# Taking 16 transposes a pair out of a four-layer graph network, and ordering its work anew with the port of GpSimd and VectorE in the plan

## The chip, the cores and the metric

One core of a Trainium2 chip. The metric is device microseconds (us) of one execution; medians of several executions are given. An execution can fall into a slower state with a lower clock. The granted TensorE clock is a share of full speed, so 1 is full. In the profile PE is TensorE's matmuls, PEld its weight loads, DVE VectorE, ACT ScalarE, POOL GpSimd, SP the engine that issues the loads. `L761` is line 761 of the kernel's file; the new kernel is longer, so its lines have other numbers.

## The reference, cut to what matters

Four residual layers on 64 graphs of 256 nodes and 256 features, fp32. The kernel works on pairs of graphs, 32 of them.

```python
h = relu(layernorm(x)); x = x + attention8(h, adj)      # layer 0: 8 heads, softmax over neighbours
h = relu(layernorm(x)); x = x + elu(gat(h, adj))        # layer 1
h = relu(layernorm(x)); x = x + gated_graph(h, adj)     # layer 2: 3 steps of a GRU cell
h = relu(layernorm(x)); x = x + gat4(h, adj)            # layer 3: 4 heads, softmax
# layer 2, one step:
m = h @ weight[i]; aggr = A.T @ m
r = sigmoid(i_r + h_r); z = sigmoid(i_z + h_z)
n = tanh(i_n + r * h_n);  h = (1 - z) * n + z * h
```

## The kernel before

The kernel lists its work as tasks (engine, expected us, what to do) and a small planner in the kernel's own file orders all tasks of all 32 pairs at build time, so that softmax and layernorm of one pair run beside the matmuls of others. After that the order on each engine is fixed.

```python
# Plan.order, at each step: the task that can begin first (cut)
for engine, us, do in t.forms:
    begin = max(start, free.get(engine, 0.0))
    for x in t.before:      # HOP, SAME: delay of a hand-over to another or to the same engine
        begin = max(begin, x.end + (self.HOP if x.engine != engine else self.SAME)[x.engine])
    key = (round(begin, 3), (t.layer == 2) == (engine == "PE"), t.pair, t.order)
...
"w4": (20, [P, T * D], FP, 6),      # 20 buffers; a pair that isn't the oldest must leave 6 of them free
```

Layer 0 leaves the softmax rows undivided and divides the context product. For that the reciprocals of the row sums are widened, transposed on TensorE (8 transposes a pair), copied out and multiplied in:

```python
rzw() <- rz() widened to 128 x 256                             # VectorE
nc.tensor.transpose(psz()[...], rzws[ti]()[:, cc] ..., ident)  # 4 a graph
nc.scalar.copy(rzT(), psz())
nc.vector.tensor_tensor(cT ..., psc, rzT, ALU.mult)
```

Each step of layer 2 has features on the partitions. The state after it is transposed to tokens (8 transposes a pair and step), after the last step as well, only to be added to `x`.

## Time and profile before

| | before |
|---|---|
| median of the first 3 runs | 4326.13 us (4325.0 to 4328.71) |
| TensorE busy | 98% |
| VectorE, ScalarE, GpSimd busy | 68%, 53%, 14% |
| granted TensorE clock, mean | 0.996 |

Most lines are in the prediction below. The list of who waited for whom on TensorE, where the first columns are the waiting group and the releaser, and the numbers are us in total, times, and the longest:

```profile
PE ps L278 <- DMA wih_sb<-in_L_gnn_w_ih_dram: 16.0, 1, 16.0
...
PE ps L909 <- ACT w L494: 10.1, 4, 5.3
...
PE ps L457 <- issue: 7.2, 1, 7.2
```

The profile's "idle" counts a gap only where no record is under way, and records overlap; so I use a second measure. **Work** is count times usual start-to-start time, summed over TensorE's groups; **waits** are what is left between the first and the last matmul. In the prediction I put the work at 4157; I had taken the mean for the context product (L614), and 10 of its 64 blocks hold a wait of 1.15 us inside. With the undisturbed 1.864 us a block it is 4147 of work and 156 of waits, and that is used from here on. (Another reading of "usual" moves some 10 us between the two columns in every kernel alike; the differences between kernels are what counts.)

### The profile page before, as it was taken

The page shows a single profiled execution, that of the slowest core. Times are in us where ns is not written, and L with a number is a line of the kernel's source. Part 1 is how long each engine was busy: PE and PEld are TensorE (multiplying, and loading weights), DVE is VectorE, ACT ScalarE, POOL GpSimd, SP SyncE. Part 2 cuts the span into 40 slices and gives each one's busy share as a digit, 9 for nine tenths or more (in the row PEclk, how much of TensorE's full clock was granted, in tenths as well). Part 3 has the DMA queues.
Part 4 walks back from the last instruction along what each step waited for, and adds up shares of the span by engine and source line. Part 5 has one row for each costly group of instructions (what it writes and reads, how often), then busy time and mean ns, then how long its engine had stood idle before and what let it go on. Part 6 is the DMA issues. An engine that isn't in the chain of part 4 may idle for free.

```text
span 4324.5 us, 56216 instructions
## 1 busy us (share of the span) xinstructions
PE 4244.1 (98%) x20720; PEld 2631.3 (61%) x20720; DVE 2930.0 (68%) x5426; ACT 2301.1 (53%) x6105; POOL 590.3 (14%) x582
## 2 busy tenths in 40 slices
PE   7999999999999999999999999999999999999997
PEld 5665566656656665666566566656655665666564
DVE  6775577667657755876676577558765765776554
ACT  4664465545545644655455456446554554564444
POOL 1111111111111111111111111111111111111111
PEclk9999999999999999999999999999999999999999
DMA  2000011000000000010000000000100100000000
GB/s 83 21 18 22 20 36 34 20 16 24 30 25 25 13 28 25 30 35 20 11 30 30 25 25 13 27 25 26 40 11 17 32 30 25 25 13 28 15 15 15
DMA packets 109986, 108.47 MB, mean 25 GB/s; under 512 B 7312, under 2 KB 109712, under 8 KB 109712
## 3 DMA queue, kind: packets, MB, share of 16 engines
q1 hardware_dynamic: 109712, 104.89, 7.6%
q8 instruction: 163, 2.67, 0.3%
q14 instruction: 111, 0.91, 0.1%
HBM read 88.09 MB, written 16.78 MB: 24 GB/s over the span
## 4 chain that ended last, share of the span: by engine, by line
PE 77%; DVE 8%; issue 8%; ACT 5%; POOL 1%; SPq 0%; DMA 0%; POOLq 0%; ACTq 0%; DVEq 0%
PE ps L761 36%; PE ps L775 7%; PE ps L518 5%; PE ps L480 5%; PE ps L573 4%; PE ps L717 3%; PE ps L654 3%; PE ps L540 2%; PE ps L457 2%; PE ps L614 2%; PE ps L840 2%; PE ps L858 2%; ACT w L886 2%; ACT w L494 2%; DVE w L823 1%
## 5 line engine op out<-in xcount | busy, mean ns | idle before, releaser
L761 PE MATMUL ps<-w,whhT 128*128 128x512 f32 x2304 | 1080.3, 595 | 0.7 <-DVE w L402 0.4
L761 PE MATMUL ps<-w,giT 128*128 128x512 f32 x2304 | 1063.6, 593 | 0.0
L494 ACT ACTIVATE w<-w,mx 128x256 f32<-128x256 f32 x1664 | 825.7, 503 | 186.3 <-DVE mx L561 128.9
L401 ACT COPY w<-ps 128x512 f32<-128x512 f32 x983 | 553.0, 587 | 657.3 <-PE ps L775 290.8
L761 PEld LDWEIGHTS ps<-w,giT 128*128 128x128 f32 x2304 | 433.6, 190 | 523.9 <-issue 513.3
L761 PEld LDWEIGHTS ps<-w,whhT 128*128 128x128 f32 x2304 | 415.3, 190 | 406.6 <-issue 383.9
L811 POOL TENSOR_TENSOR w<-w,w 128x512 f32<-128x512 f32 x192 | 251.2, 1317 | 1689.6 <-ACT w L806 1331.8
L402 DVE COPY w<-ps 128x512 f32<-128x512 f32 x553 | 366.4, 684 | 153.7 <-PE ps L573 58.0
L786 ACT ACTIVATE w<-ps,brz 128x512 f32<-128x512 f32 x192 | 131.8, 687 | 463.2 <-PE ps L761 460.3
L791 DVE TENSOR_SCALAR w<-w 128x512 f32<-128x512 f32 x192 | 81.6, 425 | 407.8 <-ACT w L786 407.7
L554 DVE SCALAR_TENSOR_TENSOR w<-ps,mask 128x512 f32<-128x512 f32 x512 | 333.3, 680 | 33.9 <-PE ps L540 33.9
L775 PE MATMUL ps<-w,w 128*128 128x256 f32 x1536 | 355.7, 379 | 0.0
L775 PEld LDWEIGHTS ps<-w,w 128*128 128x128 f32 x1536 | 286.2, 190 | 60.7 <-issue 22.9
L494 ACT ACTIVATION_READ_ACCUMULATOR w<-w,mx 128x1 f32 x1664 | 322.9, 194 | 0.0
L823 DVE SCALAR_TENSOR_TENSOR w<-w,w 128x512 f32<-128x512 f32 x192 | 152.5, 794 | 246.3 <-ACT w L818 240.7
L561 DVE TENSOR_REDUCE mx<-w 128x4 f32<-128x1024 f32 x256 | 309.2, 1208 | 2.0
L573 PE MATMUL ps<-ident,w 128*128 128x128 f32 x2048 | 269.4, 273 | 0.6
L573 PEld LDWEIGHTS ps<-ident,w 128*128 128x128 f32 x2048 | 235.1, 140 | 57.1 <-issue 25.6
L818 ACT ACTIVATE w<-ps,brz 128x512 f32<-128x512 f32 x192 | 130.8, 681 | 235.0 <-PE ps L761 234.9
L424 POOL TENSOR_SCALAR rs<-mv 128x4 f32<-128x4 f32 x128 | 33.6, 262 | 1354.8 <-DVE mv L417 1293.5
L886 ACT ACTIVATE w<-w,f 128x256 f32<-128x256 f32 x512 | 217.1, 503 | 1.4
L445 DVE TENSOR_SCALAR w<-x,mv,rs 128x256 f32<-128x256 f32 x384 | 185.3, 541 | 16.5 <-POOL rs L425 15.8
(113 smaller groups left out, 5633.0 us busy)
## 6 DMA issues: line engine op xcount, KB each, us to landing
adj<-in_adj_dram SPq DMA_DIRECT2D x128, 512.0 KB, 4.1
x<-in_x_dram SPq DMA_DIRECT2D x64, 256.0 KB, 2.8
out_dram<-x SPq DMA_DIRECT2D x64, 256.0 KB, 2.2
gg_sb<-in_L_gnn_weight_dram SPq DMA_DIRECT2D x3, 256.0 KB, 3.7
wih_sb<-in_L_gnn_w_ih_dram SPq DMA_DIRECT2D x1, 768.0 KB, 6.9
whh_sb<-in_L_gnn_w_hh_dram SPq DMA_DIRECT2D x1, 768.0 KB, 8.6
wq_sb<-in_L_gnn_Wq_dram SPq DMA_DIRECT2D x1, 256.0 KB, 2.8
wk_sb<-in_L_gnn_Wk_dram SPq DMA_DIRECT2D x1, 256.0 KB, 3.0
```

Source lines behind the costliest of these rows:

```text
L401: (A, act(n), lambda: nc.scalar.copy(dst(), src())),
L402: (V, dve(n), lambda: nc.vector.tensor_copy(dst(), src())),
L480: mm(ps()[:, c * D : (c + 1) * D], chunk(src, k, 2 * g + c), rhs[:, k, :], start=k == 0, stop=k == 1)
L494: nc.scalar.activation(tok(e(), N)[:, i, :], tok(e(), N)[:, i, :], AF.Exp, bias=mx()[:, m : m + 1], accum_out=zs()[:, z : z + 1],)
L518: mm(ps(), w[:, k, o * P : (o + 1) * P], tok(hT(), N2)[:, k, :], start=k == 0, stop=k == 1)
L554: (V, dve(N2), lambda s=s, j=j, b=b, t=t: nc.vector.scalar_tensor_tensor(tok(s(), N)[:, 2 * j : 2 * j + 2, :], tok(b(), N), SCALE, tok(mb( ...
L561: (V, dve(4 * N), lambda s=s, mx=mx, h4=h4: nc.vector.tensor_reduce(mx()[:, h4], tok(s(), N), AX.X, ALU.max, negate=True)),
L573: nc.tensor.transpose(tok(ps(), P)[:, 2 * i + c, :], tok(s(), N)[:, 2 * k + i, c * P : (c + 1) * P], ident,)
L761: mm(ps(), w[:, k, c0 : c0 + P], at_o(src, k), start=n == 0, stop=n == 2 * len(terms) - 1)
L775: mm(ps()[:, g * N : (g + 1) * N], tok(h())[:, t, o * P : (o + 1) * P], tok(am(), N)[:, t, :], start=c == 0, stop=c == 1,)
L811: (G, pool(N2), lambda o=o, u=u, hT=hT, hn=hn: nc.gpsimd.tensor_sub(at_o(u, o), at_o(hT, o), at_o(hn, o))),
L886: (A, act(N, 1), lambda t=t, g=g, h=h, e=e: nc.scalar.activation(tok(e(), N)[:, h, :], tok(sd[h // 2](), N2)[:, h % 2, g * N : (g + 1) * N ...
```

## The change

Fewer transposes, a planner that knows more, and a choice among 18 orders. The core of the diff, cut (lines left out or shortened, `...`):

```diff
+    # layer 0: divide the softmax rows, on whichever engine the planner gives it to
+    [(A, 2 * act(N, 1), lambda f=divided: f(nc.scalar.mul)),
+     (V, 2 * 0.33, lambda f=divided: f(nc.vector.tensor_scalar_mul), True)],
-    rzw, turn_rz, rzT and the multiply of the context product
+    evict(N2, ... cT ..., psc)

-        for l in range(NL):
+        for l in range(NL - 1):
...
+        # last step with tokens on the partitions: state as stationary operand, weights streamed
+        mm(out, chunk(src, k, t), w[:, k, c0 : c0 + n], ...)
+        add((V, ...tensor_tensor(at_o(rz[g], c), ps(), brz_bc, ALU.add)))   # biases now along the row
+        ...
+        add(either(lambda eng: eng.tensor_sub(two(h, g), two(h, g), two(hn, g))))
+        add(either(lambda eng: eng.tensor_add(two(xt, g), two(xt, g), two(hn, g))))

-                        begin = max(start, free.get(engine, 0.0))
+                        begin = max(start, free.get(engine, 0.0), free.get("port", 0.0) if len(form) > 3 else 0.0)
...
+                        key = (round(begin, digits), ...)
...
-    order = plan.order()
+    order = plan.best([(spare, digits) for spare in range(6, 12) for digits in (1, 2, 3)])
```

A task marked `True` takes the port: GpSimd's, and VectorE's with operands in SBUF. `best` plans once for each of 18 settings (how many of the `w4` buffers the younger pairs must leave free, and to how many decimals begin times are compared), replays each order four times with durations drawn from 0.9 to 1.15 of the expected, and keeps the order with the smallest sum. `w4` has 28 buffers, as the 4 double-size ones went. Some elementwise operations of GpSimd may now also go to VectorE (`either`).

## The prediction

> **What bounds the kernel now.** I read the page first (engine totals, groups), then TensorE's groups with their idle time, then the order in time around one repeat, and last the busy time by stretch. The totals and four groups:
>
> ```profile
> PE 4244.1 (98%) x20720; PEld 2631.3 (61%) x20720; DVE 2930.0 (68%) x5426; ACT 2301.1 (53%) x6105; POOL 590.3 (14%) x582
> ...
> L573 PE MATMUL ps<-ident,w 128*128 128x128 f32 x2048 | 269.4, 273 | 0.6
> ```
>
> ```profile
> L761 PE MATMUL ps<-w,whhT 128*128 128x512 f32 x2304 | 1080.3, 595 | 0.7 <-DVE w L402 0.4 <-DVE w L554 0.3
> ...
> L840 PE MATMUL ps<-ident,w 128*128 128x128 f32 x768 | 105.6, 277 | 13.8 <-DVE w L828 11.3 <-ACT w L606 2.5
> ...
> L600 PE MATMUL ps<-ident,rzw 128*128 128x128 f32 x256 | 39.0, 275 | 0.0
> ```
>
> TensorE is the bound: 98%, no other engine over 68%. But "mean ns of one" is a pipelined latency, not the price of one. The price is the distance from start to start:
>
> ```profile
> 2001.03 1.88 PE L761 MATMUL ps<-w,whhT 128*128 128x512 f32 x4
> 2002.75 1.88 PE L761 MATMUL ps<-w,giT 128*128 128x512 f32 x4
> ...
> 2007.90 1.04 PE L457 MATMUL ps<-ident,w 128*128 128x128 f32 x8
> 2008.77 1.04 PE L573 MATMUL ps<-ident,w 128*128 128x128 f32 x8
> 2009.65 3.73 PE L858 MATMUL ps<-w3a,w 128*128 128x264 f32 x16
> ...
> 2017.40 1.89 PE L480 MATMUL ps<-wo_sb,w 128*128 128x256 f32 x8
> 2019.13 1.45 PE L761 MATMUL ps<-w,whhT 128*128 128x512 f32 x3
> ```
>
> Four 512-column records take 1.72 us (0.429 each), eight 256-column ones 1.73 (0.216), eight transposes 0.87 to 0.88 (0.109). One fp32 product leaves two records, a transpose one.
>
> I summed count times usual start-to-start for every TensorE group of the trace: 4157 us, where the first to the last matmul takes 4303. The other 146 us are gaps: about 12 in the first pair's slice (start-up), 28 in the last pair's (nothing left to fill in), and some 3.5 us in each of the 30 other pairs. In steady state the order repeats every 397.4 us, three pairs, 132.5 us a pair:
>
> ```profile
> 810.30:1207.70 397.40, 394.34 (x1933) 244.61 (x1932) 274.44 (x506) 215.08 (x572) 55.21 (x55) 1.00 0.08 25
> 1207.70:1605.20 397.50, 394.46 (x1933) 244.63 (x1932) 274.60 (x507) 215.22 (x572) 55.24 (x55) 1.00 0.08 25
> 4189.40:4324.50 135.10, 111.34 (x442) 64.60 (x440) 64.89 (x108) 55.29 (x140) 15.23 (x14) 0.92 0.04 12
> ```
>
> (Columns: stretch, its length, busy us of PE, PEld, DVE, ACT, POOL, clock, DMA.) The last row is the drained tail. Of the 3.5 us, about 0.95 is paid on each switch into or out of the matmuls that use part of the array (L540, L614, L930), and no order saves it. So about 2.5 us a pair are waits that an order could avoid. Where one such wait comes from is seen here:
>
> ```profile
> 1243.73 1.27 POOL L811 TENSOR_TENSOR w<-w,w 128x512 f32<-128x512 f32 x1
> 1243.81 1.74 DVE L823 SCALAR_TENSOR_TENSOR w<-w,w 128x512 f32<-128x512 f32 x1 [0.46 <-POOL w L811]
> ...
> 1247.87 0.68 DVE L828 SCALAR_TENSOR_TENSOR w<-w,w 128x512 f32<-128x512 f32 x1
> ...
> 1248.61 0.98 PE L840 MATMUL ps<-ident,w 128*128 128x128 f32 x7 [0.58 <-DVE w L828]
> ```
>
> A GpSimd op starts, the VectorE op behind it takes 1.74 instead of 0.68, and five microseconds on TensorE waits for the end of that VectorE chain. The same happens once in every repeat.
>
> **What the Trainium skill says.** "SBUF — State Buffer", section "Who interferes with whom": VectorE and GpSimd share a port pair as an exclusive lock, and a VectorE op with two SBUF inputs, or a copy or tensor_scalar in a two-port mode, blocks or is blocked for a whole instruction. The trace agrees: L445, one input, 0.41 us alone, has a maximum of 1.44; L823 goes from 0.69 to 1.75. VectorE ops that read PSUM (L554, L634, L802) stay at 0.68 to 0.69 under GpSimd work. "TensorE: Matmul & The Clock Gate", section "Wait — 56ns, not 53.3ns?": 215.7 ns start to start for 512 columns, warm; an fp32 record here takes 429, near twice that. Section "Part 4: PE-mode transpose" gives some 275 ns for a transpose in context; records here are 273 to 282, but in a run they start 109 apart, and that decides. "Perfetto Trace Analysis", section "Identifying the Most-Contended Engine", warns that matmul busy time is a poor gauge of headroom; hence the sum of intervals above.
>
> **The change, part by part, in microseconds a pair (32 pairs).**
> (1) Layer 0's division moves from the context product (row sums widened, 8 transposes, an eviction, a multiply) to the softmax rows. TensorE: minus 8 x 0.109 = 0.87. Added: 32 divisions of 128x256, which the fixed order gives 20.75 to ScalarE and 11.25 to VectorE.
> (2) The last recurrent step is computed with tokens on the partitions, so its result needs no transposing back: minus another 8 x 0.109 = 0.87. Its r and z products keep shape and price (512 columns). The 4 blocks of the n gate become eight 256-column records each instead of four of 512: 1.73 for 1.72, plus 0.04.
> TensorE's work: minus 1.70 a pair, minus 54 in all, all of it on the path that sets the end.
> (3) VectorE, by start-to-start times of like ops: divisions 11.25 x 0.32 = +3.6; last step loses 2 each of L791, L795, L802, L823, L828 (6.1) and gains 16 ops of 0.6 (9.6); adds to x from PSUM -1.2, context multiply -1.2, widening -0.8, adds that leave GpSimd +0.8, reciprocals +0.5. Net about +5.2, or 166 in all: 2930 to about 3100, 73% of the new span. ScalarE: divisions 20.75 x 0.40 = +8.3, the rest about -0.5: 2301 to about 2550, 60%. Both still under TensorE, so nearly all beside it.
> (4) Order. The new one holds GpSimd and VectorE's SBUF ops apart, so the 1 us surprises of L823, L828, L707 and L445 should mostly go, and is chosen among 18 by replays with varied durations. No time of that choice is used here. I compared the two fixed orders by hand: for every TensorE block in pairs 5 to 26, the TensorE work standing between it and the block it depends on, minus the traced durations of the ops between (plus 0.17 a hop). Before, blocks fall short by 1.0 us a pair in sum, after by 0.3; asking for 0.5 us of margin, 3.3 against 2.2. So I estimate that the 2.5 us shrink by a third to two thirds: -1.2 a pair, -38 in all.
> (5) Ends: four more small loads (about 0.5 us of issue each) stand before the weights that the first transposes wait for: +2. The tail's chain trades a transpose for two or three VectorE ops: 0 to +2, taken as 1.
> Sum: 4326 - 54 - 38 + 3 = 4237. I take 4235.
>
> **Rivals.**
> A. Only the transposes count; the waits stay 2.5 a pair because busier VectorE and ScalarE make as many new ones (the division sits between the exponential and its transpose, and after the last step come more VectorE ops): 4326 - 54 + 3 = 4275. For it: VectorE at 73% has longer queues. Against: the softmax blocks have 5 us and more of other TensorE work to hide behind.
> B. Order is the main gain, waits almost vanish: a further 35 to 40 below my sum, near 4200. For it: the order's per-op figures match the trace (0.598 for a 512-element VectorE op, start to start, in both), so the port was its only large unknown. Against: waits of under 0.25 us, half of the total, are not clearly the port's.
> C. VectorE or the GpSimd lock becomes the bound: above 4326. At 73% with GpSimd at 14% I see no room for it.
> D. New gaps of several microseconds drop TensorE's clock. The granted clock is 0.996 on average now, and I see no reason for it in steady state.
>
> **Range and chances.** Rival A gives the upper half, B the lower; 8 in 10: 4206 to 4273. The 2% line is 4326/1.02 = 4241, just above my number, so faster by over 2% gets 0.57, within 2% gets 0.42, slower 0.01.
>
> **What would show it.** Transpose records fall by 512, with PE's steady work near 127.5 a pair. VectorE busy about 3100, ScalarE about 2550. Maxima of VectorE ops with SBUF operands should fall from 1.4 to 1.75 toward 0.7; if they stay, step 4 is wrong in its cause. TensorE's idle time in front of layer 3's transposes and of the recurrent step's should shrink; if it moves to the divided rows' transposes or to layer 3's entry, rival A holds. A repeat of about 129.6 us a pair confirms the sum; 130.8 is A, 128.4 is B.

## More of the kernel before

TensorE can do nothing for 16 us, until the recurrent weights have landed. It stops again for 7.2 us when the preparation is done and the first rows are not there yet (L457).

## The result, and the profile after

4248.64 us (4247.34 to 4250.05, 4 runs) against 4327.42 (4325.0 to 4328.77, 4 runs). The ratio is 0.9819, interval 0.9802 to 0.9836. Here and below a ratio is the mean time of one kernel's fast runs over that of the other's of the same rounds, so not quite the ratio of the medians quoted. The difference is under 2%, and the time is 14 us above the number predicted.

Of the page after, the totals and the transposes of the divided rows (busy us, mean ns of one, idle before):

```profile
PE 4178.7 (98%) x20720; PEld 2674.7 (63%) x20720; DVE 3061.3 (72%) x5920; ACT 2521.8 (59%) x6744; POOL 603.1 (14%) x602
...
L637 PE MATMUL ps<-ident,w 128*128 128x128 f32 x2048 | 268.2, 274 | 3.9 <-DVE w L624 1.6
```

TensorE still bounds, at the same 98%; VectorE and ScalarE rose by 131 and 221 us (166 and 250 were worked out), and neither sets the end. TensorE's idle time in front of layer 3's transposes fell from 17.7 to 7.5 us and in front of the recurrent step's from 13.8 to 2.7. In front of the divided rows' it rose from 0.6 to 3.9 only, and in front of a layer's first transposes (L457, now L505) from 13.0 to 19.5, nearly all of that at the two ends. The repeat is now five pairs in 648.5 us, 129.7 a pair (stretch, length, busy us of PE, PEld, DVE, ACT, POOL, clock, DMA):

```profile
1100.80:1749.30 648.50, 646.69 (x3223) 414.17 (x3221) 475.53 (x923) 391.87 (x1051) 95.26 (x94) 1.00 0.08 25
1749.30:2397.80 648.50, 646.68 (x3223) 414.18 (x3221) 475.37 (x923) 391.88 (x1051) 95.27 (x94) 1.00 0.08 25
```

The waits of TensorE after:

```profile
PE ps L318 <- DMA wih_sb<-in_L_gnn_w_ih_dram: 18.8, 1, 18.8
PE ps L505 <- DVE w L493: 11.3, 3, 9.9
PE ps L505 <- issue: 7.6, 1, 7.6
...
PE ps L760 <- DVE w L750: 5.8, 8, 0.8
```

The long ones are all at the two ends. Against the lines of before, the first is 2.8 longer, and a wait of 9.9 us is new. Where the 76.7 us between the two profiled spans (4324.5 and 4247.8) went:

| part | before | after | difference |
|---|---|---|---|
| work | 4146.9 | 4093.3 | -53.6 |
| waits from 140 us to 270 us before the end | 113.4 | 78.0 | -35.4 |
| waits in the first 140 us | 12.7 | 17.6 | +4.9 |
| waits in the last 270 us | 30.2 | 34.7 | +4.5 |
| first matmul at | 16.0 | 18.8 | +2.8 |

The new wait of 9.9 us, in order of time on TensorE (start us, us, operation; in brackets the idle time):

```profile
4199.75 3.61 PE L901 MATMUL ps<-giT,w 128*128 128x512 f32 x12
4213.25 2.29 PE L505 MATMUL ps<-ident,w 128*128 128x128 f32 x8 [9.89 <-DVE w L493]
```

and the same place before:

```profile
4281.57 0.27 PE L840 MATMUL ps<-ident,w 128*128 128x128 f32 x1
4284.03 0.98 PE L840 MATMUL ps<-ident,w 128*128 128x128 f32 x7 [2.19 <-DVE w L828]
4289.67 2.21 PE L457 MATMUL ps<-ident,w 128*128 128x128 f32 x8 [4.66 <-DVE w L445]
```

The last pair has no other pair to hide behind. Before, it waited 2.2 and 4.7 us with seven transposes between; now the step's whole elementwise end lies in one wait. In that end the port shows too, in GpSimd and VectorE just before:

```profile
4198.64 1.28 POOL L956 TENSOR_TENSOR x<-x,w 128x512 f32<-128x512 f32 x1
4198.84 1.62 DVE L958 SCALAR_TENSOR_TENSOR w<-w,w 128x512 f32<-128x512 f32 x1
```

VectorE's 0.68 us op takes 1.62 behind GpSimd's. So even with the port in the plan such pairs still occur: a plan that expects the block may choose it. They still stop TensorE too. The last line of the list of waits after is such a case: L750, a VectorE op of 0.68 us, has a maximum of 1.80, and in seven of those eight stops, one in nearly every repeat, TensorE waits 0.8 us behind an L750 of 1.79 to 1.80 us.

### The profile page after: what moved, and what is told of

It is laid out like the page before. It is cut to its first block, busy times and chain, and to the rows that moved or that the text cites. A ratio compares the mean times of both kernels' runs of the same rounds, so it can differ in the third digit from the quotient of the medians.

```text
span 4247.8 us, 56704 instructions
## 1 busy us (share of the span) xinstructions
PE 4178.7 (98%) x20720; PEld 2674.7 (63%) x20720; DVE 3061.3 (72%) x5920; ACT 2521.8 (59%) x6744; POOL 603.1 (14%) x602
## 4 chain that ended last, share of the span: by engine, by line
PE 92%; DVE 5%; ACT 2%; issue 0%; DMA 0%; SPq 0%; POOL 0%; POOLq 0%; DVEq 0%; ACTq 0%
PE ps L821 28%; PE ps L901 16%; PE ps L802 8%; PE ps L528 5%; PE ps L637 5%; PE ps L566 5%; PE ps L587 3%; PE ps L658 3%; PE ps L978 3%; PE ps L760 3%; PE ps L1050 3%; PE ps L505 2%; PE ps L1029 2%; PE ps L697 2%; PE ps L681 1%; PE ps L887 1%
## 5 line engine op out<-in xcount | busy, mean ns | idle before, releaser
L821 PE MATMUL ps<-w,whhT 128*128 128x512 f32 x1536 | 724.5, 596 | 3.8 <-DVE w L445 3.8
L821 PE MATMUL ps<-w,giT 128*128 128x512 f32 x1536 | 714.1, 594 | 0.0
L821 PEld LDWEIGHTS ps<-w,giT 128*128 128x128 f32 x1536 | 288.2, 190 | 344.4 <-issue 331.9
L821 PEld LDWEIGHTS ps<-w,whhT 128*128 128x128 f32 x1536 | 274.9, 191 | 247.6 <-issue 228.0
L901 PE MATMUL ps<-whhT,w 128*128 128x512 f32 (+1 forms) x1024 | 364.0, 492 | 0.0
L901 PE MATMUL ps<-giT,w 128*128 128x512 f32 (+1 forms) x1024 | 359.6, 488 | 0.0
L624 ACT ACTIVATE w<-w,rz 128x256 f32<-128x256 f32 x664 | 289.2, 502 | 50.8 <-DVE rz L615 50.7
L901 PEld LDWEIGHTS ps<-giT,w 128*128 128x128 f32 x1024 | 192.0, 190 | 152.5 <-issue 135.4
L901 PEld LDWEIGHTS ps<-whhT,w 128*128 128x128 f32 x1024 | 188.3, 192 | 106.9 <-issue 91.2
L833 ACT ACTIVATE w<-ps,brz 128x512 f32<-128x512 f32 x128 | 87.6, 684 | 252.5 <-PE ps L821 252.3
```

What stands on the lines that cost most here:

```text
L624: op(tok(s(), N)[:, i, :], tok(s(), N)[:, i, :], rz()[:, z : z + 1])
L821: mm(ps(), w[:, k, c0 : c0 + P], at_o(src, k), start=n == 0, stop=n == 2 * len(terms) - 1)
L901: mm(out, chunk(src, k, t), w[:, k, c0 : c0 + n], start=m == 0, stop=m == 2 * len(terms) - 1)
```

## The experiments

The work came out as counted. What the waits owe to is open. Theory P, mine: the plan knows the port. Rival B or S: which of the orders is taken. Rival F: the new dataflow has other chains. Each diff below is cut to its core. All twelve kernels gave the right result. In the table "setting" is spare buffers and the rounding of begin times; bold is a setting that the planner's own choice took.

| run | dataflow | port | setting | median us | work | waits | first matmul at |
|---|---|---|---|---|---|---|---|
| before | old | no | own | 4326 to 4327 | 4147 | 156 | 16.0 |
| after | new | yes | **8, 10 ns** | 4248.64 | 4093 | 130 | 18.8 |
| e1 | new | no | **11, 1 ns** | 4237.99 | 4092 | 120 | 18.1 |
| e2 | new | yes | 9, 1 ns | 4356.21 | 4094 | 235 | 18.7 |
| e3 | new | no | 9, 1 ns | 4300.95 | 4099 | 175 | 18.4 |
| e5 | new | no | 8, 10 ns | 4419.26 | 4095 | 297 | 18.3 |
| e6 | new | yes | 11, 1 ns | 4428.22 | 4099 | 303 | 18.8 |
| e4 | old | yes | **6, 1 ns** | 4297.06 | 4148 | 125 | 19.0 |
| e7 | old | no | **8, 1 ns** | 4314.78 | 4147 | 142 | 18.6 |
| e8 | tokens only | yes | **6, 10 ns** | 4299.49 | 4124 | 151 | 18.5 |
| e9 | division only | yes | **6, 10 ns** | 4307.94 | 4120 | 160 | 18.7 |

(Work, waits, the first matmul and 5 us after the last one's start add up to the profiled span, which is 1 to 4 us under the median. The work column is good to some 7 us: the kernels with the whole new dataflow stand at 4092 to 4099, since the usual distance is read from each trace.)

### e1: the port taken out of the plan

```diff
-  ... free.get("port", 0.0) if len(form) > 3 else 0.0
+  ... free.get("port", 0.0) if len(form) > 99 else 0.0     (all four places)
```

> The new kernel, but its order no longer holds GpSimd and VectorE's SBUF ops apart; still the best of 18. Theory P (the knowledge of the port saved the waits): the time comes back toward 4275, at least 4265, VectorE ops of 1.4 to 1.75 us reappear at unplanned places, and TensorE waits for VectorE more. Rival B (the choice among 18 saved them): within 5 us of 4249. Rival F (the dataflow itself, fewer blocks and other chains, saved them): within 5 us of 4249 as well.

Measured: 4237.99, ratio to before 0.9796 (0.9781 to 0.9811), 11 us faster than with the port. Theory P falls in this form, and neither rival foresaw the gain. VectorE ops that took over 0.2 us longer than usual are 123, against 86 after and 130 before, and yet TensorE waits less. The repeat is one pair, 129.3 us:

```profile
910.18 17.19 PE ps L901 x48
1039.48 17.19 PE ps L901 x48
1168.78 17.19 PE ps L901 x48
```

These are pieces of the chain that ended last; the same piece comes back every 129.3 us.

### e2, e3: one order in place of the best of 18

```diff
-    order = plan.best([(spare, digits) for spare in range(6, 12) for digits in (1, 2, 3)])
+    order = plan.best([(9, 3)])                               (e3: and the port out, as in e1)
```

> The new kernel with the port known, but one order (the 9 spare buffers of its table, begin times rounded to a nanosecond as before) in place of the best of 18. Theory P: within 8 us of 4249. Rival B: 4265 to 4285. Rival F: within 5 us of 4249.

> The new dataflow under the old way of ordering: no port, one order. Theory P and rival B: about 4275 (4326 less 54 for the transposes plus 3 for the ends), 4265 to 4290. Rival F: within 5 us of 4249.

Measured: 4356.21 and 4300.95, ratios 1.007 and 0.9941. With everything of the change but another setting, the kernel is slower than before. The setting alone is worth 108 us (e2 against after), twice what the transposes are. Both theories had the size of e2 wrong: P said 4249, and I had let rival B say 4265 to 4285. In e3 both said 4265 to 4290 and missed by 11.

### e5, e6: the two settings crossed with the port

```diff
+    order = plan.best([(8, 2)])     # e5, port out: after's setting
+    order = plan.best([(11, 3)])    # e6, port in: e1's setting
```

> The new kernel with its own setting (8 spare buffers, begin times rounded to 10 ns) held fixed, the port not known. Theory S (which of the 18 settings is taken decides, the port rule only reshuffles them): anything from 4238 to 4301, the spread seen between settings, without a common sign with the next run. Theory P, as far as it is left (the port rule helps at an equal setting): slower than 4249 by 10 or more. Rival N (the port rule costs time by itself, since it keeps VectorE waiting in the plan): about 4238, faster than 4249 by some 10.

> The port known, at the setting that the choice took without it (11 spare buffers, 1 ns). Theory S: 4249 or more, up to 4356, since the choice with the port known passed it over. Theory P: faster than 4238. Rival N: about 4248, 10 slower than without the port at this setting.

Measured: 4419.26 and 4428.22, ratios 1.0213 and 1.0234, both slower than before, e6 by over 2% clear of noise (e5's interval begins at 1.0196). At setting 8 the port rule is 171 faster, at 9 it is 55 slower, at 11 it is 190 slower. There is no common sign, as theory S said, but both times lie far above its ranges (up to 4301 and up to 4356); neither P nor N survives as a rule. With the port and without it, the setting that the replays chose was the fastest of the three measured. What the replays expect can be had by building the kernels, without a chip. The mean of the four is 4313 for e1, 4330 for after, 4372 for e3, 4441 for e2, 4490 for e5 and 4528 for e6: the order of the measured times, 71 to 100 us above them. Between e4 and e7 below (4390 and 4378, measured 4297 and 4315) they are the wrong way round.

What a bad order does is seen in e6. Its waits, and one of them on TensorE in order of time:

```profile
PE ps L1029 <- ACT w L542: 82.5, 31, 5.3
```

```profile
2754.95 1.04 PE L505 MATMUL ps<-ident,w 128*128 128x128 f32 x8
2760.36 2.17 PE L1029 MATMUL ps<-ident,w 128*128 128x128 f32 x8 [4.37 <-ACT w L542]
2763.13 2.17 PE L1029 MATMUL ps<-ident,w 128*128 128x128 f32 x8 [0.60 <-ACT w L542]
```

The same transposes in the kernel after:

```profile
1483.70 1.09 PE L1029 MATMUL ps<-ident,w 128*128 128x128 f32 x8
1484.63 0.60 PE L637 MATMUL ps<-ident,w 128*128 128x128 f32 x4
1485.29 0.66 PE L1065 MATMUL ps<-ident,w 128*128 128x128 f32 x4
1485.98 1.07 PE L1029 MATMUL ps<-ident,w 128*128 128x128 f32 x8
```

In e6 the transposes of layer 3's softmax (L1029) come with no other pair's matmuls ahead of them, TensorE waits 4.4 us for ScalarE, and then runs eight transposes in 2.17 us, twice as long: the clock dropped, as the granted clock of 0.61 in this stretch shows (columns as above):

```profile
2756.00:2768.00 12.00, 6.07 (x24) 3.33 (x26) 11.63 (x15) 12.00 (x40) 0.00 (x0) 0.61 0.00 0
```

Such a hole comes every second pair and costs about 13 us (173 us of waits more than after, over thirteen holes). I counted in the fixed orders how many TensorE blocks of one pair's layer 3 stand in a row with nothing else between, the drained last pair aside: at most 6 in after and in e1; 11 in a row in thirteen places in e6; 22 in a row, a whole layer 3, in five places in e5. The numbers of buffers and of TensorE instructions are the same, and e6 and e1 even leave the same 11 buffers free. So in the two worst orders the added waits stand where other pairs' matmuls are missing when layer 3 comes. The count doesn't explain every order: e2, with 105 us of waits more than after, has four rows of 10 or more (one of 22, three of 10), and e3, with 45 more, has none over 7. What makes their waits is not shown.

### e4, e7: the old dataflow under the new planner

All 16 transposes are back, with the buffers that they need (`w4` then has 27).

```diff
-    the divided rows; the last step in token tiles
+    rzw, turn_rz, rzT, the multiply; for l in range(NL)       (e7: and the port out)
```

> The old dataflow (all 16 transposes back in each pair) under the new ordering, port and best of 18. Theory P or B: 4327 less 35 for the waits plus 0 to 5 for the ends: 4290 to 4300. Rival F: 4320 or more. 512 more transpose records than the new kernel.

> The old dataflow, best of 18, the port not known. If the choice alone makes the gain of the waits: 4285 to 4305, as with the port (4297). If the old dataflow needs the port rule: 4315 or more.

Measured: 4297.06 and 4314.78, ratios 0.9933 and 0.9972. The first is inside its range. The second is not: it misses 4285 to 4305 by 10 and stands at the 4315 from which I had said that the old dataflow needs the port rule. The rest of the change takes 31 or 14 us of waits off the unchanged dataflow, and 3 us of that are lost at the first matmul, since both still carry the new bias loads. "The rest" is the planner together with `either` and the split of the double-size buffers, which no run takes apart. Rival F falls. In the old dataflow the rule did what it was made for: the VectorE ops of over 0.2 us more than usual are 34 in e4 and 117 in e7. With e1 this gives the port rule a gain of 18 in the old dataflow and a loss of 11 in the new: again no common sign.

### e8, e9: each half of the dataflow alone

```diff
e8:  layer 0 as before, last step in token tiles
e9:  divided rows, layer 2 as before
```

> New order, only the last step in token tiles. TensorE's work lies 27 us under that of the old dataflow (8 transposes x 0.109 x 32 = 28, less 1.5 for the narrower products), so 4297 less 27 = 4270 if waits stay equal; 4258 to 4285 with what another order may change. If the end's longer chain comes from this part, the last 70 us and the wait ahead of layer 3's first transposes look as in the new kernel (9 to 10 us), not as in the old (about 5).

> New order, only the division in layer 0. TensorE's work lies 28 us under that of the old dataflow (8 transposes x 0.109 x 32), so 4297 less 28 = 4269 if the waits stay those of the old dataflow under the new order (125 us between the first and the last matmul); 4265 to 4300 with the waits of 120 to 150 that the other chosen orders show. The end (the last 70 us) without the longer last chain: about 23 to 25 us of waits, not 27.

Measured: 4299.49 and 4307.94, ratios 0.9935 and 0.9956; both miss, 14 and 8 us above the ranges. The work fell about as counted (24 and 27 us under e4's, 27 and 28 said), but the waits of the chosen orders rose by 26 and 35. Neither half alone beats e4. A saving of work of under 1% is smaller than the draw from one chosen order to the next, here 120 to 160 us of waits; only the work column tells such halves apart.

On the end they do decide. e8's wait ahead of layer 3's first transposes:

```profile
PE ps L506 <- DVE w L494: 11.6, 3, 9.9
```

and e9's:

```profile
PE ps L505 <- DVE w L493: 5.4, 2, 4.7
```

The longest is 9.9 with the token tiles and 4.7 without. It is so in every run but e12, where that chain was changed: 9.9 in the five with token tiles and the port in the plan (after, e2, e6, e8, e10), 8.8 in the four without the port (e1, e3, e5, e11), 4.7 in the four with the old last step (before, e4, e7, e9). So the longer wait comes from the last step's form. The waits of the last 70 us were 27.0 in both e8 and after, 25.2 in e9, 24.8 and 24.9 in e4 and e7, 22.9 before. So the form is worth some 2 us there, and another 2 came with the rest of the change.

### e10, e11, e12: the ends

The recurrent weights are loaded ahead of layer 0's weights and the bias rows, and the first rows' buffers no longer share memory with the preparation's. The order on the engines in the main part is unchanged (e10: after's; e11: e1's).

```diff
+    for tag in ("x", "st", "mv", "rs"): tiles[tag] = [const.tile(...) ...]
+    tiles["w4"] = 8 of the 28 from const as well
-    wq_sb ... wo_sb, brz_bc, bhn_bc, bhh_bc loaded ahead of the recurrent weights
+    ... loaded behind them
```

> The new kernel, same order on every engine in the main part, but the recurrent weights are loaded first and the buffers of the first rows don't overlap those of the preparation. If the start is what my sum of the ends missed: TensorE's first matmul moves from 18.8 us to 12 to 15, the 7.6 us of nothing after the preparation shrink to 2 to 5, the steady stretch keeps its waits, and the time falls by 5 to 11: 4238 to 4244. If the start is hidden by something else: 4247 to 4250.

> The same early loads on the fastest order so far (port not known, 11 spare, 1 ns; 4238): 4227 to 4233, if the start's gain adds to it.

Measured: 4230.53 (ratio to before 0.9778) and 4222.83 (0.976), both better than expected, by 7 and 4 us. In e10 the steady stretch kept its waits (2.6 per 130 us in both), and the start moved. After, around the end of the preparation and at the first matmul:

```profile
44.03 0.59 PE L398 MATMUL ps<-blk,b_w 128*128 128x8 f32 x4
...
52.25 1.07 PE L505 MATMUL ps<-ident,w 128*128 128x128 f32 x3 [7.63 <-issue]
```

and in e10:

```profile
12.55 1.73 PE L312 MATMUL ps<-ident,wih_sb 128*128 128x128 f32 x7 [12.55 <-DMA wih_sb<-in_L_gnn_w_ih_dram]
```

```profile
37.32 0.59 PE L401 MATMUL ps<-blk,b_w 128*128 128x8 f32 x4
37.77 1.07 PE L509 MATMUL ps<-ident,w 128*128 128x128 f32 x8
```

6.2 us came from the first matmul, and the whole 7.6 from the preparation's end, where I had left 2 to 5. The wait also cost more than its own length: from 48 to 58 us the granted clock was 0.50 in after and 1.00 in e10, and the first eight records of layer 0's query product (L566, in e10 L570) took 4.98 and 3.70 us. e11 is the fastest kernel, 2.4% under before and also under after and e1.

e12 adds to e11 that the last step's bias joins before its last product arrives, and that the last pair's adds stay off GpSimd:

```diff
-    hn = 0.5 * hn + ps;  hn = hn + bias
+    hn = 0.5 * hn + bias;  hn = hn + ps
+    return forms[1:] if len(plan.pairs) == B // 2 else forms     # VectorE only
```

> As the run before, and the last step's bias joins before its last product comes in, and the last pair's two adds stay off GpSimd, so the last chain is 2 to 3 us shorter (the wait ahead of layer 3's first transposes 9 to 10 us, then 6 to 7). This changes the plan, so another of the 18 is taken: 4225 to 4260 by which steady waits that one has.

Measured: 4238.16, ratio 0.9794, within the range, but the plan changed with the edit and took setting 9, 1 ns, whose steady waits are higher (2.8 per 130 us against 2.2). The wait ahead of layer 3's first transposes became 8.2, where e11 has 8.8: 0.6 gained, not 2 to 3. So this repair of the end is not shown to be worth more than that.

## Why the prediction was right or wrong

The time was inside the range, and the call, nearly even between faster by over 2% and within 2%, leaned the wrong way by 7 us. By its steps:

**(1), (2) TensorE's work: right.** Minus 54 said, minus 53.6 measured, with 512 transposes fewer and the narrower products at the price of wide ones. e8 and e9 show the two halves in the work column. (The 0.95 us that the working puts on "each switch" is a pair's sum: one switch costs some 0.1 us, as the trace before has it.)

**(3) The other engines: right.** VectorE 3100 said, 3061 measured; ScalarE 2550 said, 2522 measured; both rises were put a little too high. Neither became the bound, and rival C never showed.

**(4) Order: size right, cause wrong.** Minus 38 said, minus 35.4 measured between the ends. The size came from the hand comparison of the two fixed orders. But the sentence that the 1 us surprises "should mostly go", and with them the waits, failed by the prediction's own sign: the maxima did not fall toward 0.7 (1.80, 1.75, 1.65 and 1.37 us in L750, L958, L875 and L493), GpSimd and VectorE still block one another (86 stretched ops, against 130), and without the port rule the chosen order is faster still. What took its place is the choice among 18: at equal work the waits run from 120 to 303 us by setting and port rule. With one fixed setting the same change could have come out at 4356 or 4428, both outside the range, and 4428 is slower by over 2%, which had got 0.01. The prediction was written with the chosen order at hand, and without that it would have needed a much wider range. That the comparison came within 3 us may be in part luck: it was not tried on e2, e5 or e6, so it is not shown that it sees a bad order.

**(5) The ends: the term that was mis-sized.** Plus 3 said, plus 12.2 measured: 2.8 at the first matmul (2 said), 4.9 in the waits of the first 140 us and 4.5 in those of the last 270 us (together 1 said). This is most of the 14 us between 4235 and 4249; the rest is the waits' 3 and the rounding from 4237. I counted the last chain's ops but not that the block of transposes in its middle had been splitting one long wait in two, nor did I look at the first pairs' order at all.

**Rivals.** A (4275) and B (4200) both missed; a repeat of 129.7 us a pair, 129.6 said, stands between them. B's repeat of 128.4 was not reached by any order whose repeat was read: e1, faster than after, has 129.3. D, a dropping clock, I dismissed for the steady state; that held for the order taken (1.00 in its repeats), but it is real in the bad orders (0.61 in e6's hole) and at the start (0.50 after the wait of 7.6 us).

What stays open: why the port rule helps one setting and hurts the next. The runs show that no sign is common, not which early decision of the planner leads into which repeat. Open too are the 4.9 us more of waits in the first 140 us, which e10 removes together with others, and what `either` and the split buffers do by themselves.

## What to carry to other kernels

When a greedy planner lays out the instructions, a small change of its settings can be worth more than the work that was saved: measure several orders of the same work, and judge a saving by the work column and the waits apart. In the two worst orders the missing filler matmuls in front of a softmax that waits for other engines made the waits, so count how many dependent blocks stand in a row before looking for a shared resource to blame. The first and the last 100 us have no other pair to hide behind, and there loads and chain length cost their full time: 18 us came back from the order of the loads and the placing of buffers alone.

## What the Trainium skill lacked or had wrong

- "TensorE: Matmul & The Clock Gate", "Part 4: PE-mode transpose", gives about 275 ns as a transpose's duration in context. The records agree (273 to 282 ns), but what removing one saves is the distance from start to start in a run, 109 ns, which the section doesn't give: worked out with it, 512 of them are worth 56 us, not 141, and the work fell by 53.6.
- The same page's start-to-start of 215.7 ns for 512 columns has no fp32 time beside it, nor a pointer to where another page counts the passes of fp32. Here an fp32 product leaves two records of 0.429 us each, 0.86 us in all, and a transpose one.
- "SBUF — State Buffer", "Who interferes with whom", is right about the lock (VectorE ops of 0.68 us took 1.6 to 1.8 behind GpSimd). It doesn't say that planning around it need not pay: with the lock in the plan the best of 18 orders took 4249 us, without it 4238; in the old dataflow 4297 and 4315.
- "Perfetto Trace Analysis", "Optimization Strategy", reads a gap that repeats as a possible lack of SBUF or PSUM. Here, with the same buffers, as many of them left free and the same work, the repeating gap came and went with the order of the instructions alone (e1 and e6: 120 and 303 us of waits).
